# B and C of the small Mamba fetched by one transfer per tile

## The chip, the cores and the metric

The kernel runs on one core of a Trainium2 chip. The core has five engines that work through their own lists of instructions in order and signal each other: TensorE (matmuls; PE in the profile, with PEld its weight loads), VectorE (DVE), ScalarE (ACT), GpSimd (POOL) and SyncE (SP), which issues most of the transfers. Sixteen DMA engines carry the transfers between the device memory and the on-chip memory, which has 128 partitions. The metric is the device time of one execution in microseconds, as the median of several runs.

## The reference

A metaformer of two layers works on 8 images of 256 channels and 32 x 32 points. Layer 0 is a Vim block (a Mamba over the 1024 points of each image, 512 inner channels) and a mixture of eight experts of which each token uses two. Layer 1 splits the channels: 128 pass through, three times 32 go through small depthwise convolutions, and the last 32 go through a small Mamba with 64 inner channels and 16 states; then a feed-forward block works on the better half of the tokens. The part around the change is the scan of the small Mamba:

```python
dA = jnp.exp(delta[..., None] * A)
dBu = delta[..., None] * Bm[:, :, None, :] * u[..., None]

def step(h, inputs):
    dA_t, dBu_t, C_t = inputs
    h = h * dA_t + dBu_t
    y = jnp.sum(h * C_t[:, None, :], axis=-1)
    return (h, y)
```

Delta and u have one value per channel and point. `Bm` and `Cm` have one value per state and point, the same for all 64 channels of an image.

## The kernel before, in words

All values are float32. The work is cut into 16 units (8 images, two halves of 512 points each) for layer 0, and into four groups of two images (four units) for everything after it: `route`, `scatter`, `experts`, `combine`, `taps_of`, `mamba_in`, `mamba_scan`, `mamba_out`, `assemble`, `ranks`, `feed_forward`, `finish`.

Both Mambas use `scan_pair`. It handles two states at once for 128 partitions of channels and 512 points. GpSimd multiplies `dtx` (delta times u) by a tile of B rows into a `dbu` tile (line 780, 128 x 1024). For each of the two states ScalarE makes the decay (line 785), VectorE scans (line 788), ScalarE copies the last column as the state for the other half (line 792), and VectorE multiplies by a tile of C rows (line 793). GpSimd adds the two states for some pairs (line 797), and TensorE adds the result into the `y` tile in its accumulators (line 804). `dbu` has four buffers.

The rows of B and C lie in a small device-memory buffer, `rows`. As every channel of an image needs the same row, a tile `bc` of 128 x 1024 is filled by a transfer that repeats two rows of 512 points over the partitions. `bc` has four buffers, used in order. For layer 0 (line 839) all 128 partitions are channels of one image, so one transfer of 512 KB fills a tile, and a pair of tiles (B and C) serves two calls of `scan_pair`.

In the small Mamba the 128 partitions are 64 channels of each of the group's two images. Before, image 0 has partitions 0 to 63 and image 1 partitions 64 to 127: `twice` makes block-diagonal weights for that. `rows` has 64 rows there: image 0's B (16), its C (16), then image 1's B and C. `mamba_scan` loops over eight pairs of states and two halves of the points, 16 calls of `scan_pair` per group. Each uses its own pair of tiles, and a tile is filled by two transfers from line 1416, one per image, each to 64 partitions and of 256 KB. One step `fetch` issues both, with a planned cost of 0.8 us on SyncE.

The order of all instructions is made at build time. Functions add steps to a `Flow`, each with an engine, an assumed time, a priority (a position in the sequence), and the buffers it reads and writes. `Flow.run` plays the steps through with these assumed times, and writes each engine's list in the order it finds: on each engine the most urgent step that can start, or one that fits before it. Buffers are handed out in the same play. So an assumed time costs nothing on the chip, but changes which step is placed next. The planner also puts placeholder matmuls (lines 525 and 529) where it sees TensorE idle for more than 0.7 us, and a table load on ScalarE where its function set changes. The default assumed time of a transfer's issue is 0.4 us.

SyncE's list holds the tiles of both Mambas (lines 839 and 1416), expert weights (1127), expert inputs and outputs (1088, 1187), and the rows of `combine`, `assemble`, `feed_forward` and `finish`. GpSimd's list also holds the indirect transfers of `scatter` (1068), `combine` (1250) and `finish` (1621).

Of the kernel before, what the change touches and what calls it, by code (L numbers as in the profile page):

```python
# [36 lines left out]
P = 128  # L37
B, C, L = 8, 256, 1024
N = 512
KC = C // P  # L40
DI0, DI1, DS, DR0 = 512, 64, 16, 16
# [131 lines left out]
class Flow:  # L173
# [29 lines left out]
    def dma(self, prio, kb, run, reads=(), writes=(), fills=(), claims=(), us=0.4):  # L203
        return self.step(SP, us, prio, run, reads, writes, fills, claims, lat=2.3 + kb / 180)
# [94 lines left out]
def layers(g, ctx, x, a, out):  # L299
    tc, nc = g.tc, g.nc  # L300
    w = ctx.enter_context(tc.tile_pool(name="w0", bufs=1))
    p = ctx.enter_context(tc.tile_pool(name="p0", bufs=1))

    def load(shape, src, tag):
        t = g.t(w, shape, tag)
        nc.sync.dma_start(t, src)
        return t
# [3 lines left out]
    def load_late(shape, src, tag):  # L311

        t = g.t(w, shape, tag)
        late_loads.append(lambda: nc.sync.dma_start(t, src))
        return t
# [17 lines left out]
    w_z = load([P, KC, DI0], a["W_in"].rearrange("(k p) n -> p k n", p=P)[:, :, DI0:], "w_z")  # L333
# [67 lines left out]
    ch1 = load_late([P, 23], a["ch1"], "ch1")  # L401
# [7 lines left out]
    w_x1 = load_late([P, 6 * DS], a["w_x1"], "w_x1")  # L409
    w_dt1 = load_late([5, P], a["w_dt1"], "w_dt1")  # L410
    w_out1 = load_late([P, 2 * GC], a["w_out1"], "w_out1")
# [31 lines left out]
    step, dma = flow.step, flow.dma  # L443
# [54 lines left out]
    def buf(name, line=None):  # L498
        b = Buf(pool[name], line)
        if line is not None:  # L500
            line.bufs.append(b)
        return b
# [270 lines left out]
    def paired(i, sp):  # L773

        return (sp + 1) * PAIRED[i] // (DS // 2) > sp * PAIRED[i] // (DS // 2)
# [34 lines left out]
    def start_y(y, skips, xs, prio):  # L810
        def go(n):
            nc.tensor.matmul(y.v[:, n], skips[n], xs.v[:, n], start=True, stop=False)
            if n == 0:
                live[0] = y

        for n in range(2):
            step(PE, 0.9, prio, lambda n=n: go(n), [xs], fills=[y])

    def end_y(y, sz, prio):
        for n in range(2):  # L820
            step(DVE, 0.72, prio, lambda n=n: nc.vector.tensor_tensor(
                sz.v[:, n], sz.v[:, n], y.v[:, n], ALU.mult), [y], [sz])
# [581 lines left out]
    def mamba_scan(n, pos):  # L1404
        grp = groups[n]
        state, y = buf("state1"), buf("y")
        start_y(y, [skip1, skip1], grp["xs"], pos)
        for sp in range(DS // 2):
            for hf in range(2):
                both = buf("bc"), buf("bc")  # L1410
                for j in range(2):

                    def fetch(j=j, hf=hf, sp=sp, both=both):
                        for i in range(2):
                            at = i * 2 * DS + j * DS + 2 * sp
                            nc.sync.dma_start(
                                both[j].v[i * DI1 : (i + 1) * DI1],
                                grp["rows"][hf].v[at : at + 2].partition_broadcast(DI1),
                            )

                    dma(pos + 2 * sp + hf - 6, 512, fetch, [grp["rows"][hf]], [both[j]], us=0.8)
                scan_pair(
                    pos + 2 * sp + hf, grp["dt"], grp["dtx"], hf, *both, y,
                    lambda j, sp=sp: neg_a1[:, 2 * sp + j : 2 * sp + j + 1],
                    (state, lambda j, sp=sp: state.v[:, 2 * sp + j : 2 * sp + j + 1]) if hf else None,
                    None if hf else (state, lambda j, sp=sp: state.v[:, 2 * sp + j : 2 * sp + j + 1]),
                    sp == DS // 2 - 1, paired(len(units) + n, sp),
                )
        end_y(y, grp["sz"], pos + DS)
# [235 lines left out]
    for i, s in enumerate(UNIT_AT):  # L1665
# [10 lines left out]
        if i % 4 == 3:  # L1676
            n = i // 4
            at = PLAN[n]
# [5 lines left out]
            m = at["mamba"]  # L1684
# [35 lines left out]
def _layout(i):  # L1720

    import numpy as np

    f = {k: np.asarray(v) for k, v in i.items()}
    c0 = {k[8:]: v for k, v in f.items() if k.startswith("L0_conv_")}
    m0 = {k[7:]: v for k, v in f.items() if k.startswith("L0_ffn_")}
    c1 = {k[8:]: v for k, v in f.items() if k.startswith("L1_conv_")}
    m1 = {k[7:]: v for k, v in f.items() if k.startswith("L1_ffn_")}

    def chunks(v):  # L1730

        return v.reshape(-1, P, v.shape[-1]).transpose(1, 0, 2)

    def columns(*vs):
        return np.concatenate([v.reshape(len(v), -1) for v in vs], 1)

    def twice(v):

        n, m = v.shape
        t = np.zeros((2 * n, 2 * m), v.dtype)  # L1740
        t[:n, :m] = v
        t[n:, m:] = v
        return t

    taps_a = np.zeros((4 * GC, len(TAPS_A) + 1), np.float32)
    taps_b = np.zeros((2 * GC, len(TAPS_B) + 1), np.float32)
    for i in range(2):
        rows = slice(i * GC, (i + 1) * GC)  # L1750
        for n, (dy, dx) in enumerate(TAPS_A):
            if abs(dx) <= 1:
                taps_a[rows, n] = c1["w_hw"][:, 0, dy + 1, dx + 1]
            if dy == 0:
                taps_a[2 * GC + i * GC : 2 * GC + (i + 1) * GC, n] = c1["w_w"][:, 0, 0, dx + 5]
        for n, (dy, dx) in enumerate(TAPS_B):
            taps_b[rows, n] = c1["w_h"][:, 0, dy + 5, 0]
        taps_a[rows, -1] = c1["b_hw"]
        taps_a[2 * GC + i * GC : 2 * GC + (i + 1) * GC, -1] = c1["b_w"]
        taps_b[rows, -1] = c1["b_h"]  # L1760

    w12 = np.concatenate(
        [
            m0["W1"].reshape(E, KC, P, HE).transpose(0, 2, 1, 3).reshape(E, P, -1),
            m0["b1"].reshape(E, FC, P).transpose(0, 2, 1),
            m0["W2"].reshape(E, FC, P, C).transpose(0, 2, 1, 3).reshape(E, P, -1),
        ],
        2,
    )

    w12f = np.concatenate(
        [
            m1["w1"].reshape(KC, P, 2, HE).transpose(2, 1, 0, 3).reshape(2, P, -1),
            m1["b1"].reshape(2, FC, P).transpose(0, 2, 1),
            m1["w2"].reshape(2, FC, P, C).transpose(0, 2, 1, 3).reshape(2, P, -1),
        ],
        2,
    )

    b2 = np.zeros((P // 32, 4, E, 4, C), np.float32)  # L1780
    for j in range(4):
        b2[:, j, :, j] = m0["b2"]
    b2 = b2.reshape(P, 4, C)

    w_x = np.zeros((DI0, 4 * DS), np.float32)
    w_x[:, :DR0] = c0["W_x"][:, :DR0]
    w_x[:, 2 * DS :] = c0["W_x"][:, DR0:]

    w_x1 = np.zeros((P, 6 * DS), np.float32)
    w_x1[:, :4] = twice(c1["x_proj_w"][:2].T)  # L1790
    w_x1[:, 2 * DS :] = twice(c1["x_proj_w"][2:].T)
    ch1 = columns(c1["conv1d_w"][:, 0], c1["A_log"], c1["conv1d_b"], c1["dt_proj_b"], c1["D"])
    ln1 = columns(c1["ln_g"], c1["ln_b"])
    a = {
        "x": f["x"],
        "W_in": c0["W_in"],
        "ch0": chunks(columns(c0["conv_w"], c0["A_log"], c0["conv_b"], c0["b_dt"], c0["Dp"])),
        "ln0": chunks(columns(c0["ln_w"], c0["ln_b"])),
        "W_x": chunks(w_x),
        "W_dt": np.concatenate([c0["W_dt"], c0["b_dt"][None]]),  # L1800
        "W_out": c0["W_out"],
        "gate_w": m0["gate_w"],
        "gate_b": m0["gate_b"],
        "W_outT": c0["W_out"].T,
        "b2": b2,
        "W12": w12,
        "W12f": w12f,
        "taps_a": taps_a,
        "taps_b": taps_b,
        "w_xm": twice(c1["in_proj_w"][:DI1].T),  # L1810
        "w_z": twice(c1["in_proj_w"][DI1:].T),
        "conv1T": np.concatenate([c1["conv1d_w"][:, 0].T] * 2, 1),
        "w_x1": w_x1,
        "w_dt1": np.concatenate([twice(c1["dt_proj_w"].T), np.tile(c1["dt_proj_b"], 2)[None]]),
        "w_out1": twice(c1["out_proj_w"].T),
        "ch1": np.concatenate([ch1, ch1]),
        "ln1": np.concatenate([ln1, ln1]),
        "wr": m1["wr"].reshape(-1),
        "br": m1["br"],
        "fb2": m1["b2"][None],  # L1820
    }
    return {k: np.ascontiguousarray(v) for k, v in a.items()}
# [15 lines left out]
```

## Time and profile before

| | us |
|---|---|
| median of three runs | 3854.12 |
| lowest and highest of the three | 3846.69, 3867.57 |
| the profiled execution's own time | 3870.05 |
| its span, first to last instruction | 3868.2 |
| TensorE busy | 3299.0 |
| VectorE busy | 2978.3 |
| GpSimd busy | 2327.8 |
| ScalarE busy | 2207.2 |
| mean time of one GpSimd product of the scans (line 780) | 2.368 |
| mean time of one VectorE scan (line 788, with a state) | 1.282 |
| mean time of one VectorE product (line 793) | 0.691 |

In the profile a line number such as L780 is a line of the kernel. A wait is shown as the instruction that waited, an arrow, and what released it; SPq stands for SyncE's list. The page has 256 transfers of 256 KB from `rows` to `bc` (line 1416, from 2328.9 to 3642.3 us) beside 512 of 512 KB (line 839, from 51.0 to 2874.4 us). The four scans of the small Mamba stand at about 2329 to 2430, 2857 to 2985, 3263 to 3379 and 3535 to 3643 us of the span. TensorE's granted clock is 0.940 of full speed over the span.

### The profile page before, as it was taken

What the parts mean: (1) busy time and instruction counts of PE and PEld (TensorE: products, weight loads), DVE (VectorE), ACT (ScalarE), POOL (GpSimd) and SP (SyncE); (2) the same over time, 40 slices, a digit from 0 to 9 for tenths busy, and PEclk for the clock granted to TensorE, in tenths of its full rate; (3) what the DMA queues carried; (4) which work ended last, traced back from release to release, by engine and by line L of the source; (5) the groups of instructions that cost most, each with busy time, mean ns of one, the idle gap of its engine ahead of it and who ended that gap; (6) DMA issues with size and microseconds to landing.
All of it is one profiled execution on the core that took longest, in us unless ns stands there. A gap on an engine that the chain in (4) does not pass through costs nothing. (4 is left out here: it accounts for less than half of the span.)

```text
span 3868.2 us, 38209 instructions
## 1 busy us (share of the span) xinstructions
PE 3299.0 (85%) x10818; PEld 1849.4 (48%) x10818; DVE 2978.3 (77%) x4281; ACT 2207.2 (57%) x4010; POOL 2327.8 (60%) x1587
## 2 busy tenths in 40 slices
PE   8888888788889888978997798988987889799768
PEld 3333333333544444434553444554555666566446
DVE  4899899989679978976898898779787527557751
ACT  4555565465757557645765665665764456556433
POOL 3567567588577768866775886545765433424522
PEclk9999999999999999998999999999888989899989
DMA  6333333344544435535553558654669666967955
GB/s 232 122 123 131 114 131 132 106 151 162 200 139 167 165 129 194 181 111 172 172 174 122 195 181 226 204 184 136 200 204 223 222 213 214 243 215 215 247 175 168
DMA packets 277073, 676.67 MB, mean 175 GB/s; under 512 B 33063, under 2 KB 114349, under 8 KB 276862
## 3 DMA queue, kind: packets, MB, share of 16 engines
q1 hardware_dynamic: 258430, 623.88, 51.2%
q0 software_dynamic: 18432, 50.36, 4.1%
q8 instruction: 87, 1.43, 0.2%
q14 instruction: 124, 1.02, 0.1%
HBM read 572.92 MB, written 101.19 MB: 174 GB/s over the span
## 5 line engine op out<-in xcount | busy, mean ns | idle before, releaser
L780 POOL TENSOR_TENSOR dbu<-dtx,bc 128x1024 f32<-128x1024 f32 x576 | 1359.3, 2368 | 515.6 <-PE y L804 349.0
L804 PE MATMUL y<-dbu,ident 128*128 128x512 f32 x1564 | 822.6, 635 | 217.9 <-POOL dbu L797 185.7
L785 ACT ACTIVATE mm<-dt,neg_a 128x512 f32<-128x512 f32 x1152 | 770.3, 688 | 208.2 <-DVE dbu L793 190.4
L788 DVE TENSOR_TENSOR_SCAN mm<-mm,dbu 128x512 f32<-128x512 f32 x576 | 703.9, 1222 | 229.7 <-ACT mm L785 153.8
L793 DVE TENSOR_TENSOR dbu<-mm,bc 128x512 f32<-128x512 f32 x1152 | 796.4, 691 | 81.4 <-DMA bc<-rows 18.0
L788 DVE TENSOR_TENSOR_SCAN mm<-mm,state,dbu 128x512 f32<-128x512 f32 x576 | 738.2, 1282 | 59.5 <-POOL dbu L780 38.7
L797 POOL TENSOR_TENSOR dbu<-dbu 128x512 f32<-128x512 f32 x370 | 480.9, 1301 | 299.4 <-DVE dbu L793 291.3
L804 PEld LDWEIGHTS y<-dbu,ident 128*128 128x128 f32 x1564 | 281.6, 197 | 560.5 <-POOL dbu L797 278.7
L1179 PE MATMUL mm<-we,hid 128*128 128x256 f32 x1984 | 486.4, 398 | 36.0 <-ACT state L792 13.0
L792 ACT COPY state<-mm 128x1 f32<-128x1 f32 x576 | 91.4, 160 | 731.6 <-DVE dbu L793 710.9
L1157 PE MATMUL mm<-xbt,we 128*128 128x256 f32 x1984 | 474.3, 391 | 30.4 <-DMA we<-in_W12f 10.4
L1179 PEld LDWEIGHTS mm<-we,hid 128*128 128x128 f32 x1984 | 387.8, 199 | 156.3 <-issue 47.4
L1157 PEld LDWEIGHTS mm<-xbt,we 128*128 128x128 f32 x1984 | 383.4, 196 | 139.2 <-issue 46.9
L525 PE MATMUL y<-still 128*128 128x512 bf16 x1059 | 275.7, 395 | 0.0
L721 PE MATMUL mm<-pre,w_tap 128*128 128x512 f32 (+3 forms) x512 | 240.8, 612 | 28.6 <-ACT pre L708 27.3
L440 ACT ACT_TABLE_LOAD x176 | 225.8, 1283 | 3.1
L1250 POOL DMA_INDIRECT ys<-slots_y,slot x128 | 122.2, 954 | 160.0 <-PE mm L1262 69.0
L1163 ACT ACTIVATE hid<-mm,we 128x256 f32<-128x256 f32 x496 | 196.8, 475 | 37.8 <-PE mm L1157 29.1
L525 PEld LDWEIGHTS <-still 128*128 128x128 bf16 x1059 | 105.9, 101 | 192.6 <-issue 118.8
L721 PEld LDWEIGHTS mm<-pre,w_tap 128*128 128x128 f32 x512 | 95.5, 193 | 166.8 <-issue 103.9
L1068 POOL DMA_INDIRECT slots_x<-xg,slot x128 | 129.8, 1014 | 68.4 <-DVE acc_b L1323 31.2
L1621 POOL DMA_INDIRECT ys<-y,slot_t x64 | 63.1, 986 | 158.7 <-DVE xc L1631 59.0
(251 smaller groups left out, 3983.6 us busy)
## 6 DMA issues: line engine op xcount, KB each, us to landing
bc<-rows SPq DMA_DIRECT2D x512, 512.0 KB
bc<-rows SPq DMA_DIRECT2D x256, 256.0 KB
we<-in_W SPq DMA_DIRECT2D x92, 514.0 KB
we<-in_W SPq DMA_DIRECT2D x92, 512.0 KB
xb<-slots_x SPq DMA_DIRECT2D x92, 256.0 KB
slots_y<-xo SPq DMA_DIRECT2D x92, 256.0 KB
we<-in_W12f SPq DMA_DIRECT2D x32, 514.0 KB
xc<-x SPq DMA_DIRECT2D x64, 256.0 KB
```

The source lines that it names most:

```text
L440: nc.scalar.preload_act_table_set(tables[name])
L525: nc.tensor.matmul(live[0].v[:, 0], still, wide, start=False, stop=False)
L721: nc.tensor.matmul(tc_.v[:, cut:], w_tap[:, c, j], pre.v[:, cut + j : j + N], start=j == 3, stop=j == 0)
L780: gpsimd(2.45, prio, lambda: nc.gpsimd.tensor_tensor(dbu.v, dtxs.v[:, n : n + 1].to_broadcast(wide2), bt.v, ALU.mult), [dtxs, bt], [dbu], ...
L785: step(ACT, 0.69, prio, lambda j=j, h=h: nc.scalar.activation(h.v, dts.v[:, n], AF.Exp, scale=scales(j)), [dts], [h], table="exp", scan=True)
L788: step(DVE, 1.25, prio, lambda j=j, h=h: nc.vector.tensor_tensor_scan(h.v, h.v, dbu.v[:, j], 0.0 if initial is None else initial[1](j), AL ...
L793: step(DVE, 0.68, prio, lambda j=j, h=h: nc.vector.tensor_tensor(dbu.v[:, j], h.v, ct.v[:, j], ALU.mult), [h, ct], [dbu], scan=True)
L797: gpsimd(1.3, prio + 2.3, lambda: nc.gpsimd.tensor_tensor(dbu.v[:, 0], dbu.v[:, 0], dbu.v[:, 1], ALU.add), [], [dbu])
L804: nc.tensor.matmul(y.v[:, n], g.ident, dbu.v[:, j], start=False, stop=stop and (paired or j == 1))
L1157: nc.tensor.matmul(tv[:, f], we[0].v[:, at : at + P], xbt.v[:, k], start=k == 0, stop=k == KC - 1)
L1163: nc.scalar.activation(hid.v[:, f], tv[:, f % 2], func, bias=we[0].v[:, at : at + 1])
L1179: nc.tensor.matmul(to, hid.v[:, f, h * P : (h + 1) * P], we[1].v[:, f * C : (f + 1) * C], start=extra is None and f == 0, stop=f == FC - 1,)
```

## The change

The channels of the two images take turns on the partitions: partition 2c holds channel c of image 0, and partition 2c + 1 channel c of image 1. The host lays out the small Mamba's weights, biases and scales in that order (`turns`). A transfer can then walk over channels first and over the two images second, and fills the whole tile at once. The step `fetch` issues one transfer, with the default assumed time.

```diff
                     def fetch(j=j, hf=hf, sp=sp, both=both):
-                        for i in range(2):
-                            at = i * 2 * DS + j * DS + 2 * sp
-                            nc.sync.dma_start(
-                                both[j].v[i * DI1 : (i + 1) * DI1],
-                                grp["rows"][hf].v[at : at + 2].partition_broadcast(DI1),
-                            )
-
-                    dma(pos + 2 * sp + hf - 6, 512, fetch, [grp["rows"][hf]], [both[j]], us=0.8)
+
+                        at = j * DS + 2 * sp
+                        rows = grp["rows"][hf].v.rearrange("(i m) n -> i m n", i=2)[:, at : at + 2]
+                        nc.sync.dma_start(both[j].v.rearrange("p s n -> p (s n)"), rows.rearrange(
+                            "i s n -> i (s n)").unsqueeze(0).to_broadcast([DI1, 2, 2 * N]))
+
+                    dma(pos + 2 * sp + hf - 6, 512, fetch, [grp["rows"][hf]], [both[j]])
...
+    turns = np.arange(P).reshape(2, DI1).T.reshape(-1)
...
-        "w_xm": twice(c1["in_proj_w"][:DI1].T),
-        "w_z": twice(c1["in_proj_w"][DI1:].T),
-        "conv1T": np.concatenate([c1["conv1d_w"][:, 0].T] * 2, 1),
-        "w_x1": w_x1,
-        "w_dt1": np.concatenate([twice(c1["dt_proj_w"].T), np.tile(c1["dt_proj_b"], 2)[None]]),
-        "w_out1": twice(c1["out_proj_w"].T),
-        "ch1": np.concatenate([ch1, ch1]),
+        "w_xm": twice(c1["in_proj_w"][:DI1].T)[:, turns],
+        "w_z": twice(c1["in_proj_w"][DI1:].T)[:, turns],
+        "conv1T": np.concatenate([c1["conv1d_w"][:, 0].T] * 2, 1)[:, turns],
+        "w_x1": w_x1[turns],
+        "w_dt1": np.concatenate([twice(c1["dt_proj_w"].T), np.tile(c1["dt_proj_b"], 2)[None]])[:, turns],
+        "w_out1": twice(c1["out_proj_w"].T)[turns],
+        "ch1": np.concatenate([ch1, ch1])[turns],
```

## The prediction

> **What bounds the kernel now.** I read the page first: its first section, its transfers by kind, then who waits for whom.
>
> ```profile
> span 3868.2 us, 38209 instructions
> ...
> PE 3299.0 (85%) x10818; PEld 1849.4 (48%) x10818; DVE 2978.3 (77%) x4281; ACT 2207.2 (57%) x4010; POOL 2327.8 (60%) x1587
> ...
> bc<-rows SPq DMA_DIRECT2D x512, 512.0 KB
> bc<-rows SPq DMA_DIRECT2D x256, 256.0 KB
> ```
>
> No engine is full over the span; what matters is each stage. The 256 transfers of 256 KB are the half tiles of the small Mamba, in four stretches (groups 0 to 3). Busy time by stretch, columns PE, PEld, DVE, ACT, POOL, then granted clock, DMA share and GB/s; the second line is an ordinary scan stretch, the sixth a stretch without scans, the last the tail:
>
> ```profile
> 2329.00:2430.00 101.00, 84.12 (x254) 43.97 (x252) 79.77 (x97) 57.63 (x96) 61.84 (x39) 0.95 0.85 216
> 2435.00:2678.00 243.00, 209.67 (x747) 130.28 (x748) 195.90 (x345) 155.18 (x326) 131.52 (x86) 0.94 0.58 190
> ...
> 2857.00:2985.00 128.00, 105.15 (x366) 71.10 (x364) 95.76 (x117) 66.07 (x118) 70.56 (x39) 0.88 0.86 220
> ...
> 3263.00:3379.00 116.00, 89.19 (x334) 63.08 (x332) 60.24 (x63) 69.46 (x118) 51.01 (x30) 0.90 1.01 246
> 3379.00:3535.00 156.00, 147.56 (x605) 101.70 (x605) 89.55 (x282) 84.62 (x189) 54.33 (x58) 0.95 0.64 202
> 3535.00:3643.00 108.00, 80.85 (x301) 48.73 (x300) 87.01 (x81) 66.90 (x117) 69.63 (x45) 0.92 0.98 263
> 3643.00:3868.00 225.00, 173.50 (x760) 124.06 (x760) 82.97 (x261) 78.52 (x162) 55.84 (x65) 0.89 0.57 179
> ```
>
> In the four stretches the DMA engines are 0.85 to 1.01 busy for 216 to 263 GB/s; in the ordinary scan stretch 0.58 gives 190. Busy share per GB/s is 0.0039 against 0.0031, so the same byte costs about 29% more engine time where half tiles fly. Packets of 4096 bytes in the trace average 261, 260, 280 and 251 ns in the four stretches and 198 in the ordinary one.
>
> Who waits on these tiles (waits, one answer per stretch: total us, times, longest):
>
> ```profile
> POOL dbu L780 <- DMA bc<-rows: 25.5, 8, 5.7
> ...
> POOL dbu L780 <- DMA bc<-rows: 17.4, 8, 5.1
> ...
> POOL dbu L780 <- DMA bc<-rows: 44.8, 11, 8.9
> DVE mm L788 <- POOL dbu L780: 39.6, 12, 5.6
> ...
> POOL dbu L780 <- DMA bc<-rows: 23.2, 7, 5.3
> ```
>
> That is 110.9 us of GpSimd waiting for B tiles, and behind it the scans on VectorE. The chain that ended last passes through it just before the tail (start, us, what):
>
> ```profile
> 3610.55 5.07 DMA bc<-rows
> ...
> 3626.12 7.80 DMA bc<-rows
> 3634.09 2.36 POOL dbu L780
> 3636.46 0.44 SPq L1416
> 3636.96 8.91 DMA bc<-rows
> ```
>
> The three landings are 21.8 us of the last 36 before GpSimd resumes. So late B tiles are on the path in the fourth scan.
>
> [...] in the quietest pairs the first half lands 3.4 us after its issue, the second 4.4 us after that same issue, where a whole tile of line 839 lands in 3.3. [...] No transfer of this form is in the trace.
>
> **The change part by part.** *Issue.* Removed: 256 issues at line 1416 of median 498 ns (128 x 2 x 0.498 = 127 us of SP). Added: 128. Nearest rows: whole tile at line 839, 320 ns; the store at line 1474, whose pattern also joins two dimensions into 256 rows, 525 ns. I take 0.53, so 68 us; bounds 0.32 and 1.0 (no gain). SP saves some 59 us, about 15 per scan, but is itself mostly waiting for free buffers, so the saving counts only as 0.5 us earlier landing per tile. Behind each issue on SP stand expert weights (line 1127), x rows and stores; all move up.
>
> *Landing.* From the first half's issue to the last completion mark of the second I find medians of 6.7, 6.4, 9.7 and 8.4 us in the four scans; a whole tile of line 839 between 2400 and 2900 us takes 4.9. I take 5.2 in the first two (in the trace a half tile's first packet starts 1.25 us after issue, line 839's at 0.97) and 6 in the last two, which carry more traffic: 1.5, 1.2, 3.7 and 2.4 less. With the 0.5 of the issue ahead, the waits shrink by 8 x 2.0 = 16, 8 x 1.7 = 14, 11 x 4.2 capped at 44, and 7 x 2.9 = 20: 94 of 110.9 us of GpSimd's waiting.
>
> *What reaches the end.* Scan 0: VectorE waited for GpSimd 8.9 us there, about a third of GpSimd's waiting, so 6 of 16. Scan 1: half, 7; group 3's routing stands among its steps, so it counts. Scan 2: the experts of group 3 run beside it on TensorE, which is idle 27 of 116 us; the following stretch is 95% busy, so at most 27 - 6 = 21 can be won, of which I take 14. Scan 3: the chain above runs through it; three landings at 5.2 to 6 save 4 to 6 us in its last 36, the whole scan some 15 of its 20. Next late there would be TensorE's sums, freeing the dbu buffers. Sum: 42 us.
>
> *Host permutation.* The weights' rows and columns stand in another order with their shapes unchanged, so every load, matmul and scan that uses them is the same size: nothing, and it needs no cover.
>
> *Order.* The transfer's planned cost falls from 0.8 to the default 0.4, and the planner places everything after the first half tile anew. The two built programs are alike up to there; scans 2 and 3 stand alike on VectorE. Between them the largest move is at the gathers of combine 1 (line 1250, before: 2592 to 2654 us). Before, 4 GpSimd products of the scan, 10 VectorE scans and 33 parts of the ranking stand among them; after, 1, 4 and none (12 further ranking parts stood ahead, now none). So on VectorE 6 x (1.25 + 0.69) = 12 us and 45 x 0.6 = 27 us (0.35 to 0.75 each, and 0.08 to read the sum) of work move behind the combine: 39 us. Without scans among them, 32 gathers took 53 us (group 3) instead of 62. VectorE was busy 51 of 65 us there and would be busy some 12 of 50; if it stays the limit to the end of unit 15, that costs 39 - 15 = 24 us. It is 83% busy from 2704 to 2857, so part is absorbed: I take 14, bounds 0 and 39. Queued behind those in-order statistics are the scans, and behind these the sums on TensorE. Also 59 more placeholder matmuls (lines 525, 529) at 0.395 us each (line 525's row on the page), 23 us, in gaps of the plan: 2, bounds 0 and 23.
>
> Sum: -42 + 16 = -26 us on the profiled execution, whose span is 3868.2 and whose time is 3870.05, 0.4% above the median 3854.12 of the three runs. Against the median: 3828.
>
> **The rivals.** *Hidden anyway:* the tiles land earlier, but TensorE (85% busy) and freed dbu buffers (349 us of GpSimd waiting on the whole page) set the pace, and only scan 3's 15 us arrive, eaten by the order: about 3854. For it: TensorE is 95% busy in the stretch at 3379. Against: the chain above. *Slower:* the pile-up at combine 1 costs its whole 39 us, and as its gathers now stand three scans earlier, GpSimd waits for the last expert rows (4.2 us before, 20 if experts are no faster). Then +59, minus 15 from scan 3 and 20 from scans 1 and 2 together: 3878. It decides once the idle time added there exceeds the 42 us that my sum wins elsewhere. For it: the order is certain, only its price is not. *All of it arrives:* 94 - 16 = 78 us: 3776. Against: neighbours' limits above. *The transfer uses few engines* or costs over 1 us to issue: [...] on 2 engines a tile's 128 packets of 0.198 us take 12.7 us, the 32 tiles of a scan 406 instead of its some 113, so four scans add 1170: about 5020. With one issue of 1.0 us alone, nothing is lost against two of 0.5.
>
> **How the numbers follow.** 0.5%, 19 us, is about what a measurement here can tell from no change. Chances: the likeliest 0.42 (its own range 3805 to 3845), hidden 0.27, slower 0.20, all of it 0.09, few engines 0.02. The likeliest lies above 3835 in a sixth of its cases (0.07 same, 0.35 faster); hidden spreads as 0.05 faster, 0.19 same, 0.03 slower; the slower rival as 0.02 same, 0.18 slower. Sums: faster 0.49, same 0.28, slower 0.23. The range from 3785 to 3882 leaves out about half of "all of it", the last rival and a tail of the slower one.
>
> **What would show it.** Right: 128 transfers of 512 KB at about 0.53 us of issue, landing in 5 to 6 us; GpSimd's waits for B tiles under 30 us; DMA share in the four stretches at 0.65 to 0.8; the four scans shorter by 5 to 20 us each. Wrong: landing still at 7 or more, or VectorE idle over 30 us at combine 1 with unit 15 ending later than 2874 us.

## The result, and the profile after

The changed kernel takes 3825.14 us as the median of four runs (3807.65 to 3828.46), against 3859.68 for the kernel before in four. The ratio is 0.99, with a 95% interval of 0.9864 to 0.9936. The profiled execution took 3825.63 us, with a span of 3823.9; before it was 3870.05 with 3868.2. So 44 us are gone between the two profiles. They start unequal: the first tile of the small Mamba was issued at 2328.9 us before and at 2338.9 after, though all instructions up to there are the same. In the thirteen profiles that share these instructions that first part took 2318 to 2347 us, and the granted clock of TensorE in it went from 0.954 to 0.956 in the three shortest to 0.947 in the longest. So one pair of profiles can't show a difference of ten microseconds; the medians have to.

The page after, its first lines and its transfers:

```profile
span 3823.9 us, 38122 instructions
...
PE 3298.0 (86%) x10877; PEld 1845.8 (48%) x10877; DVE 2964.8 (78%) x4281; ACT 2210.1 (58%) x4013; POOL 2330.2 (61%) x1589
...
bc<-rows SPq DMA_DIRECT2D x640, 512.0 KB
```

The engines do the same work as before to within 0.5% (TensorE 3299.0 and 3298.0). The 256 half transfers have become 128 whole ones (640 with the 512 of layer 0). The issue took what the nearest row had suggested (the transfers of one line, durations in ns: least, median, most):

```profile
L1417 SPq DMA_DIRECT2D bc<-rows x128: 512/524/1271, 2338.9 to 3601.4; - x128
```

The stretches of the four scans, the two between scans 2 and 3 and after scan 3 among them (columns PE, PEld, DVE, ACT, POOL, then granted clock, DMA share, GB/s):

```profile
2339.00:2424.00 85.00, 77.93 (x240) 40.45 (x239) 76.82 (x96) 55.98 (x95) 62.70 (x37) 1.00 0.79 256
...
2860.00:2968.00 108.00, 94.32 (x332) 62.60 (x331) 89.82 (x107) 62.31 (x109) 68.25 (x37) 0.89 0.72 236
...
3247.00:3350.00 103.00, 89.00 (x352) 64.02 (x351) 58.30 (x62) 71.19 (x121) 50.69 (x30) 0.93 0.83 285
3350.00:3502.00 152.00, 142.69 (x594) 99.56 (x592) 89.88 (x282) 84.23 (x187) 54.01 (x58) 0.97 0.64 202
3502.00:3601.00 99.00, 81.80 (x296) 49.10 (x296) 83.30 (x81) 64.00 (x114) 68.80 (x45) 0.90 0.86 285
3601.00:3824.00 223.00, 172.04 (x764) 121.94 (x762) 83.87 (x262) 80.44 (x166) 57.92 (x66) 0.91 0.57 182
```

Each scan is shorter, from its first tile's issue to its last: 101.1 to 85.1 us, 128.5 to 108.4, 115.1 to 103.2, 106.7 to 99.0. The DMA engines are less busy (0.72 to 0.86, before 0.85 to 1.01) and move more (236 to 285 GB/s, before 216 to 263). The stretch after scan 2 and the tail have nearly kept their lengths (156 and 152, 225 and 223). Packets of 4096 bytes in the four stretches average 204, 197, 191 and 201 ns; before, 261, 260, 280 and 251. A tile lands, by the median from its first issue to its last completion mark over the tiles whose marks are all in the trace, in 5.4, 5.0, 6.2 and 6.1 us; before, in 6.7, 6.4, 9.7 and 8.4.

GpSimd's waits for B tiles, one line for each of the four scans:

```profile
POOL dbu L780 <- DMA bc<-rows: 14.8, 8, 5.6
...
POOL dbu L780 <- DMA bc<-rows: 11.7, 6, 4.2
...
POOL dbu L780 <- DMA bc<-rows: 22.5, 9, 4.9
DVE mm L788 <- POOL dbu L780: 11.6, 3, 5.3
...
POOL dbu L780 <- DMA bc<-rows: 16.9, 10, 3.8
```

Their sum is 65.9 us, where it was 110.9. VectorE's wait behind GpSimd in scan 2 fell from 39.6 to 11.6. The chain that ended last can be followed back only to 3607.6 us in this profile, 6 us after the last tile was issued, so it doesn't tell whether a tile is still on it. In the profile of the new transfer in the old order (below) the chain still passes through a landing of 7.40 us in scan 3.

### The profile page after: what moved, and what is told of

It reads as the page before. It is cut to its first block, busy times and chain, and to the rows that moved or that the text cites. A ratio compares the mean times of both kernels' runs of the same rounds, so it can differ in the third digit from the quotient of the medians.

```text
span 3823.9 us, 38122 instructions
## 1 busy us (share of the span) xinstructions
PE 3298.0 (86%) x10877; PEld 1845.8 (48%) x10877; DVE 2964.8 (78%) x4281; ACT 2210.1 (58%) x4013; POOL 2330.2 (61%) x1589
## 3 DMA queue, kind: packets, MB, share of 16 engines
q14 instruction: 123, 1.01, 0.1%
## 5 line engine op out<-in xcount | busy, mean ns | idle before, releaser
L525 PE MATMUL y<-still 128*128 128x512 bf16 x1112 | 292.7, 397 | 0.0
```

What stands on the lines that cost most here:

```text
L525: nc.tensor.matmul(live[0].v[:, 0], still, wide, start=False, stop=False)
```

## The experiments

My theory: the whole-tile transfer makes the gain, because half tiles in one block of 64 partitions are slow, and the new order that the planner finds gives some of it back. The rivals: the order makes the gain; the smaller number of transfers and issues makes it. The ratios below are against the kernel before, measured on the same chip beside each set.

### The transfer and the order apart

The planned cost moves no work on the chip, only the order. So two kernels complete a square: the new transfer in the old order, and the old transfer in the new order. For the first, the lists of TensorE, VectorE, ScalarE and GpSimd are those of before, entry by entry; for the second, those of the changed kernel.

```diff
-                    dma(pos + 2 * sp + hf - 6, 512, fetch, [grp["rows"][hf]], [both[j]])
+                    dma(pos + 2 * sp + hf - 6, 512, fetch, [grp["rows"][hf]], [both[j]], us=0.8)
```

> The changed kernel with the planned cost of 0.8 us put back: one whole transfer per tile, but every engine's list as in the kernel before (SyncE's too, with one entry where two stood). If the whole-tile transfer makes the gain and the new order costs some 10 us of it, 3815 us, 45 below before, with packets of 4096 bytes at about 205 ns in the four scans. If the new order makes the gain, 3860 as before. If both share it, some 3840.

Measured: 3807.63 us in six runs, ratio 0.9865 (0.9842 to 0.9888): 52 us faster. Packets took 204, 193, 181 and 197 ns in the four scans. The theory's figure was 45. The four scans of this kernel:

```profile
2337.00:2428.00 91.00, 81.05 (x246) 42.32 (x245) 79.47 (x97) 56.88 (x96) 61.64 (x39) 0.98 0.73 240
...
2855.00:2965.00 110.00, 93.56 (x357) 64.86 (x358) 97.69 (x116) 65.84 (x118) 69.92 (x38) 0.94 0.78 263
...
3238.00:3331.00 93.00, 82.16 (x330) 59.16 (x329) 58.14 (x62) 67.96 (x115) 50.48 (x30) 0.98 0.88 309
...
3485.00:3589.00 104.00, 83.25 (x294) 50.95 (x293) 90.07 (x80) 64.06 (x113) 71.54 (x45) 0.85 0.80 270
```

For the second, the same cost is taken from the kernel before:

```diff
-                    dma(pos + 2 * sp + hf - 6, 512, fetch, [grp["rows"][hf]], [both[j]], us=0.8)
+                    dma(pos + 2 * sp + hf - 6, 512, fetch, [grp["rows"][hf]], [both[j]])
```

> The kernel before with the planned cost of 0.4 us: two half transfers per tile, in the order of the changed kernel. If the transfer makes the gain and the order costs, 3865 to 3880 us. If the order makes the gain, 3825. Landing of a tile as in the kernel before, 6.4 to 9.7 us in the four scans, either way.

Measured: 3867.21 us in 22 runs, ratio 1.0038 (1.0024 to 1.0051): 15 us slower. Packets of 4096 bytes stayed at 252 to 267 ns, and a tile landed in 6.3, 6.9, 10.0 and 8.0 us. So the transfer makes the whole gain and the order none of it.

One thing moves along with the gain: the granted clock. It averaged 0.9455 over the six runs of the new transfer in the old order and 0.9408 over the 27 runs of the kernel before beside them; the old transfer in the new order had 0.9415. Among those 27 a run with 0.001 more clock was 2.9 us shorter, by a straight line through them. As an estimate from these, some 14 of the 52 us go with the clock. Chance at the start is not the reason, as the common first part had 0.950 in the new transfer's profile and 0.954 in the kernel before. Whether shorter waits raise the granted clock, or a higher clock shortens the scans, no run separates.

### What about the transfer: its number, or where it writes

Two transfers per tile as before, with 64 rows of 4096 bytes each, in the old order. Only the partitions differ, and with them the host's order of the weights: one image on the even, one on the odd.

```diff
-                                both[j].v[i * DI1 : (i + 1) * DI1],
+                                both[j].v.rearrange("(c i) s n -> i c s n", i=2)[i],
```

> Two transfers of 256 KB per tile as before, in the order of before, but with the images on alternate partitions, so that each half goes to every second partition over all 128 instead of to one block of 64. If blocks of 64 partitions make the packets slow, 4096 byte packets fall from 250 to 280 ns to about 205, a tile lands in 5.5 to 6.5 us, and the time is 3820 to 3835. If the number of transfers and issues is what costs, packets and landing stay as before and so does the time, 3855 to 3865.

Measured: 3804.40 us in five runs, ratio 0.9867 (0.9846 to 0.9888), the same as one whole transfer and better than the 3820 to 3835 expected. Packets took 194, 195, 178 and 198 ns, tiles landed in 5.4, 5.5, 6.1 and 5.8 us. The four scans of this kernel:

```profile
2335.00:2426.00 91.00, 81.03 (x248) 42.49 (x248) 80.00 (x98) 57.22 (x96) 61.88 (x38) 0.98 0.72 240
2850.00:2960.00 110.00, 94.05 (x355) 64.88 (x354) 98.11 (x116) 65.78 (x118) 69.67 (x38) 0.93 0.79 263
3233.00:3325.00 92.00, 82.31 (x332) 59.64 (x330) 59.04 (x63) 68.36 (x117) 50.86 (x30) 0.98 0.90 313
3475.00:3578.00 103.00, 81.51 (x300) 50.09 (x298) 88.50 (x81) 65.00 (x114) 70.87 (x46) 0.88 0.83 273
```

So the second issue and the second transfer cost nothing that can be measured. The opposite trial keeps the new layout, with the channels in turns, but writes each tile in two blocks of 64 partitions:

```diff
+                        parts = 2 if n in (0, 1, 2, 3) else 1
+                        m = P // parts
+                        for k in range(parts):
+                            nc.sync.dma_start(
+                                both[j].v[k * m : (k + 1) * m].rearrange("p s n -> p (s n)"),
+                                rows.rearrange("i s n -> i (s n)").unsqueeze(0).to_broadcast([m // 2, 2, 2 * N]))
```

> The changed layout (channels in turns) in the order of before, but each tile filled by two transfers, one to partitions 0 to 63 and one to 64 to 127. If blocks of 64 partitions are the cause, this is as slow as the kernel before, 3845 to 3860 us, with packets at 250 ns or more. If the layout itself, or the image of the source alternating, were the cause, it is fast, some 3805.

Measured: 3852.33 us in 14 runs, ratio 1.0003 (0.9982 to 1.0023). All of the gain is gone, and the DMA share is back:

```profile
2339.00:2439.00 100.00, 87.53 (x253) 45.50 (x252) 81.43 (x97) 57.36 (x96) 61.34 (x39) 0.91 0.86 218
2864.00:2985.00 121.00, 99.30 (x366) 67.72 (x364) 93.98 (x117) 66.11 (x118) 71.03 (x39) 0.93 0.89 235
3261.00:3373.00 112.00, 87.67 (x332) 62.12 (x331) 59.81 (x63) 68.88 (x117) 51.07 (x30) 0.91 1.02 259
3525.00:3636.00 111.00, 82.32 (x300) 49.73 (x298) 84.26 (x80) 66.35 (x116) 68.30 (x45) 0.89 0.96 256
```

The block of partitions is the cause: with it the kernel is slow in either layout (ratios of 1 and 1.0003), and without it fast with one transfer or with two (0.9865 and 0.9867). The blocks tried are 0 to 63 and 64 to 127; one that lies across them, such as 32 to 95, was not.

### The blocks by themselves

Five series of transfers, each 8 MB, stand ahead of the kernel before. All read one row of x repeatedly.

```diff
+    def half(to):
+        nc.sync.dma_start(to, point.partition_broadcast(DI1))
...
+    for i in range(32):
+        half(lone[i % 4][:DI1])
+    for i in range(32):
+        half(lone[i % 4][DI1 * (i % 2) : DI1 * (i % 2) + DI1])
+    for i in range(32):
+        half(lone[i % 4].rearrange("(c i) n -> i c n", i=2)[0])
+    for i in range(32):
+        half(lone[i % 4].rearrange("(c i) n -> i c n", i=2)[i % 2])
+    for i in range(16):
+        nc.sync.dma_start(lone[i % 2], point.partition_broadcast(P))
```

> The kernel before with five series of transfers ahead of all other work, each 8 MB in pieces of 4096 bytes, the tiles holding their bytes overwritten later: 32 halves all to partitions 0 to 63; 32 halves to 0 to 63 and 64 to 127 in turn; 32 halves all to even partitions; 32 halves to even and odd partitions in turn; 16 whole tiles. [...] the first runs at some 200 GB/s with packets near 300 ns, the second between that and the rest, and the last three at 300 GB/s or more with packets under 200 ns. If blocks are not the cause, all five run alike.

Measured, one stretch from inside each series in that order (the last two columns are DMA share and GB/s):

```profile
6.00:38.00 32.00, 0.00 (x0) 0.00 (x0) 0.00 (x0) 0.00 (x0) 0.65 (x3) 1.00 1.04 211
44.00:73.00 29.00, 0.00 (x0) 0.00 (x0) 0.00 (x0) 0.00 (x0) 0.00 (x0) 1.00 1.04 239
80.00:106.00 26.00, 0.00 (x0) 0.00 (x0) 0.00 (x0) 0.00 (x0) 0.00 (x0) 1.00 0.85 263
111.00:137.00 26.00, 0.00 (x0) 0.00 (x0) 0.00 (x0) 0.00 (x0) 0.00 (x0) 1.00 0.78 263
143.00:173.00 30.00, 0.00 (x0) 0.00 (x0) 4.11 (x21) 0.26 (x1) 0.00 (x0) 1.00 0.78 260
```

This was one execution, and in the last series loads of the kernel itself stand between the whole tiles. Packets of 4096 bytes take 318, 280, 208, 192 and 198 ns in the mean. Their median is 159 in the last three and 318 in the first, which is twice as long. In the first two series the engines are full (a share of 1.04, which counts overlapping packets) at 211 and 239 GB/s. The rate of the first is 0.80 of the highest (211 to 263). In the last three series the engines have room (0.78 to 0.85); what sets the rate there, no run shows. The 300 GB/s expected of them did not come, so the series show a limit for the blocks, and only a lower bound without them.

### The number of engines

The layout of before with one transfer per tile, which has to walk over the images first:

```diff
...
+                        nc.sync.dma_start(both[j].v.rearrange("p s n -> p (s n)"), rows.rearrange(
+                            "i s n -> i (s n)").unsqueeze(1).to_broadcast([2, DI1, 2 * N]))
```

> One transfer per tile with the channels of each image in one block of partitions, as in the kernel before: its source walks over the two images first. [...] landing 15 to 30 us after issue, and the kernel takes 4500 to 5100 us. If that dimension does not matter, it runs like the one transfer in turns, 3810 to 3830.

Measured: 4825.71 us in one run. A tile lands in 27.3 us by the median, though a packet takes 168 ns in the first scan, where the DMA share is only 0.18. The line's issues and what waited for it:

```profile
L1416 SPq DMA_DIRECT2D bc<-rows x128: 482/3411/12947, 2318.0 to 4577.7; - x128
...
who waited for it (us, times):
  POOL dbu L780: 1082.9, 63
  DVE dbu L793: 469.7, 62
```

The issue alone takes 3.4 us by the median, where it was 0.5. As an estimate from these, a tile's 128 packets are 128 x 0.168 = 21.5 us of packet time over a landing of 27.3 us, so 0.8 packets at a time; in the changed kernel's first scan they are 128 x 0.204 = 26.1 us over 5.4 us, so 4.8 at a time. How many engines they had is not shown, as the trace does not name the engine of a packet. That this form is slow is measured, and the turns of the images avoid it: a tile lands in 5.0 to 6.2 us in the changed kernel.

### Which scans carry the gain

The old order and the new layout, with whole tiles in two groups and block halves in the other two (the run with block halves above is their common base):

```diff
+                        parts = 2 if n in (2, 3) else 1
+                        m = P // parts
+                        for k in range(parts):
...
```

> As the run with block halves, but with whole tiles in the scans of groups 0 and 1. By the prediction's sum these two scans are worth 13 of 42 us on the path: 3830 to 3842. If the gain of the first scans is lost before the end because other engines set the pace there, 3850; if they carry half or more, 3825 to 3830.

> As the run with block halves, but with whole tiles in the scans of groups 2 and 3. By the prediction's sum these are worth 29 of 42 us: 3815 to 3825. If the late scans carry nearly all, 3805 to 3810; if the parts do not add up, the two runs' gains together miss the 46 to 52 us of the whole.

Measured: groups 0 and 1, 3833.37 us in 22 runs, ratio 0.9949 (0.9932 to 0.9965), 20 us; groups 2 and 3, 3831.09 us in 22 runs, ratio 0.9937 (0.9920 to 0.9954), 24 us. Together 44, against 52 for all four with an interval of 43 to 61: the parts add up within what is measured. The late pair misses the 3815 to 3825 expected of it.

### Where the order costs

The old transfer lost 15 us by the order. I had put such a loss at combine 1, and the trace has what I described there. VectorE's work between the first and the last gather of combine 1, in the kernel before, the changed one, and the changed one in the old order; for the last two also the stretch from there to the end of unit 15:

```profile
2592.00:2654.00 62.00, 54.32 (x191) 32.18 (x190) 49.13 (x136) 36.87 (x96) 44.06 (x40) 0.89 0.55 177
```

```profile
2577.00:2636.00 59.00, 52.87 (x173) 30.48 (x172) 16.72 (x44) 34.74 (x86) 34.74 (x36) 0.91 0.54 173
2636.00:2877.00 241.00, 212.37 (x711) 121.34 (x709) 215.71 (x342) 156.95 (x261) 165.59 (x103) 0.94 0.54 173
```

```profile
2592.00:2652.00 60.00, 50.37 (x188) 30.65 (x187) 49.71 (x136) 36.24 (x94) 43.75 (x39) 0.94 0.59 181
2652.00:2871.00 219.00, 190.00 (x607) 111.03 (x605) 189.34 (x236) 143.97 (x236) 151.72 (x94) 0.91 0.55 178
```

VectorE is busy 16.7 of 59 us there after the change, where it was 49.1 of 62. The moved work makes the stretch behind the gathers 22 us longer than in the old order (241 and 219). But the gathers also end 18 us sooner, counted from the first small-Mamba tile (297 and 315 us). So unit 15's last tile is issued 537.5 us after that first tile in the changed kernel and 534.3 in the old order: only 3 us are lost by then. Two runs tell the place apart. They have the new order only after combine 1, or only up to it:

```diff
+                    dma(pos + 2 * sp + hf - 6, 512, fetch, [grp["rows"][hf]], [both[j]], us=0.8 if n == 0 else 0.4)
```

> The changed kernel with the planned cost of 0.8 us for group 0's tiles and 0.4 us for the others: every list is as in the kernel before up to the second small scan, so combine 1 keeps its scans and ranking parts, and only the order after it changes. If the order costs its 14 us at combine 1, this is as fast as the run with the old order, some 3805 us; if it costs them later, it is like the changed kernel, some 3822.

> The opposite: 0.4 us for group 0's tiles, 0.8 us for the others. Every list is as in the changed kernel up to the second small scan, with combine 1's gathers and statistics ahead of scans and ranking, and planned with the old cost from there. If the order costs its 14 us at combine 1, some 3822 us; if later, some 3805.

Measured: order new only late, 3807.38 us in five runs, ratio 0.9886 (0.9867 to 0.9905); new only early, with combine 1's pile-up, 3798.57 us in seven, ratio 0.9870 (0.9851 to 0.9889). The pile-up costs nothing that can be measured: 0.9870 against 0.9865 with the old order. The late order costs 8 us by the medians (0.9886 against 0.9865), but the intervals overlap, so no cost is shown. Two other planned costs of the new transfer, 0.55 and 1.0 in place of 0.8, give two more orders:

> The changed kernel with a planned cost of 0.55 us, near the measured issue. Its lists are nearly those of the changed kernel on VectorE (31 places differ), those at combine 1 too: some 3822 us if combine 1 costs. If small differences of order scatter the time by as much as 14 us, anywhere from 3805 to 3840.

> The changed kernel with a planned cost of 1.0 us. Its lists are nearly those of the kernel before on VectorE (16 places differ, all late), combine 1 as there: some 3805 us if combine 1 is what costs; 3800 to 3825 if late differences scatter the time.

Measured: 3812.15 us in four runs, ratio 0.9893 (0.9871 to 0.9916), and 3802.07 us in four, ratio 0.9863 (0.9837 to 0.9888). Six orders with a fast transfer lie between 0.9863 and 0.9900. The changed kernel, at 0.9900, has only four runs, and its interval (0.9864 to 0.9936) covers five of the six ratios, and the sixth (0.9863) is at its edge. So an order that costs 15 us with the slow transfer costs, by the medians, between nothing and some 13 with the fast one, and where is not settled. The profiles name one place to look: scan 2 takes 102 to 103 us in the three kernels with the new late order (the changed one, the late one, cost 0.55) and 92 to 93 in the four with the old late order (old order, spread halves, early, cost 1.0). What follows it is shorter by about 8 us in the mean of the first three, so most of that comes back. Four orders have medians of 3798 to 3808 us: the old, the early, the late and that of cost 1.0. None is shown to beat the changed kernel, and the lowest, 3798.57, came with the highest mean clock, 0.949.

## Why the prediction was right or wrong

The forecast was 3828 against a median of 3854.12, 26 us or 0.7% less; measured were 3825.14, and 34.5 us or 1.0% less (0.6 to 1.4%) than the four runs of the kernel before, 3859.68. The direction and the cause were right, and several terms were not. That the sum came so near is in part luck: the gain was too small by 10 us, the errors of its four parts partly cancel, and the term for the order stood at the wrong place.

**What bounds the kernel.** Right: half tiles in one block of 64 partitions made the packets slow. The run in blocks (1.0003) and the run on alternate partitions (0.9867) show it apart from layout and count. In the lone series one block ran at 211 GB/s with a median packet of 318 ns; without blocks it was 260 to 263 GB/s and 159 ns. Why a block is slow, and what holds the others at 263, no run shows.

**Issue.** The duration was right (0.53 taken, 0.524 measured). Its value was wrong: the 0.5 us per tile that I added to each landing gain is worth nothing measurable, as two issues on alternate partitions are as fast as one (0.9867 and 0.9865). So it was not the number of halves that cost here. The quiet pairs, with the second half landing 1 us after the first (4.4 and 3.4 us), could not tell a cost of the second transfer from slow blocks.

**Landing.** 5.2 and 6 us taken, 5.4, 5.0, 6.2 and 6.1 measured. Right. The DMA share was not quite: I gave 0.65 to 0.8, and the last two scans have 0.83 and 0.86.

**GpSimd's waits.** Wrong: I let each wait shrink by the whole gain of its tile, from 110.9 to 17, and forecast under 30. They are 65.9. I argue, without a run for it, that a faster scan asks for its next tile sooner, so that the wait partly refills: the four scans together are 56 us shorter, and the waits 45.

**What reaches the end.** The sum was 42 us, the transfer alone brought 52 (43 to 61). Its split was off: scans 0 and 1 are worth 20 us (13 to 26), not 13; scans 2 and 3 are worth 24 (18 to 31), not 29. In the old order, two profiles of the fast transfer (whole tiles, spread halves) against two of the slow one (the kernel before, block halves) show the four scans 10, 15, 21 and 5 us shorter in the mean; I had taken 6, 7, 14 and 15. The first three were taken too small and scan 3 too large. There I read from the chain that late B tiles set the pace, but behind the tiles VectorE has 90 us of work in the 104 us that scan 3 then takes, so little more could be won. What I left out of the sum is other traffic: in scan 2 the expert weights of line 1127 landed in 9.7 us by the median before and in 5.5 after. That this is where the missing gain of scan 2 lies is argued, not shown.

**Order.** The size, 16 us, is near what the order costs with the old transfer, 15. Its place was wrong: combine 1 idles VectorE as described (16.7 us busy of 59), and nothing measurable comes of it, as the kernel with that pile-up and the old order later is as fast as any. Two steps failed. I let the gathers shrink by 15 us without scans among them; they took 59 us, where they had taken 62. And I let the work moved behind them delay the end of unit 15. It does lengthen that stretch by 22 us, but the scans that moved behind the gathers also let the gathers end 18 us sooner, which I had not counted. My sign of being wrong came true to the letter, with VectorE idle for 42 us at combine 1 and unit 15's last tile at 2876.5 us, after 2874. It was a bad sign: this execution had already begun the small Mamba 10 us later, and from its first tile on unit 15 ends 8 us sooner than before (537.5 and 545.5).

**The rivals.** "Hidden anyway" fell: the scans of groups 0 and 1 alone bring 0.5%. "Slower" had a real loss in it, but with the wrong place and too large a price. "All of it arrives" did not come either: the transfer alone brought 52 us where that rival counted 94. "Few engines" was not shown, as no trace names the engine of a packet; the form nearest to it is the kernel with the image outermost, which costs 970 us in one run. The 1170 I had for it was an estimate that assumed two engines.

## What to carry to other kernels

A transfer that writes a block of 64 partitions can be slow though its pieces are large: packets of 4096 bytes took 251 to 280 ns in the mean here, and 191 to 204 in the changed kernel, which has no such block. Look at the mean packet in the stretch, or at the DMA share per GB/s, before counting issues. If a tile has two halves with different sources, let them take turns on the partitions: each transfer then spreads over all 128 partitions instead of one half of them, and one transfer can do both. Here it walked over the 64 channels first (3807.63 us in the old order); with the two images first it took 4825.71. Where a planner makes the order, put the old assumed time back once, to see apart what the change did and what the new order did.

## What the runs showed that I had not expected

The lone series outside the blocks ran at 260 to 263 GB/s with DMA engines that were not full (shares of 0.78 to 0.85), where I had expected 300 or more. The granted clock rose with the faster transfer (0.9455 and 0.9408). Two transfers per tile in place of one, 128 more issues of half a microsecond each, made no difference (0.9867 and 0.9865). VectorE could stand idle for 42 us of the 59 at combine 1, and nothing measurable was lost at the end.
